# Attention of a graph network on one core: the turned one-hots move from VectorE to ScalarE, and VectorE weighs seven tiles of a block instead of five

## The chip, the cores and the metric

The kernel runs on one core of a Trainium2 chip, as one program in one launch. The metric is the device time of an execution in microseconds. Before the change it is 14080.11 us, the median of four runs (14073.81 to 14083.2).

## What is computed

A graph has 20,000 nodes with 256 features and 340,000 directed edges, self loops among them. Layer 0 is two relational graph convolutions with eight edge types, a residual and a layer norm. Layer 1, which the change touches, is attention with four heads over the edges into each node (`row`) from its neighbours (`col`):

```python
def _gat_forward(x, W, a_l, a_r, edge):
    h = (x @ W).reshape(n, NHEAD, OUT_F)
    hl = jnp.sum(a_l * h, axis=-1)
    hr = jnp.sum(a_r * h, axis=-1)
    e = jax.nn.leaky_relu(hl[row] + hr[col], negative_slope=ALPHA)
    e_max = jax.ops.segment_max(e, row, num_segments=n)
    ee = jnp.exp(e - e_max[row])
    denom = jax.ops.segment_sum(ee, row, num_segments=n)
    att = ee / denom[row]
    msg = att[:, :, None] * h[col]
    out_h = jax.ops.segment_sum(msg, row, num_segments=n)
    return out_h.reshape(n, NHEAD * OUT_F)
x = _layernorm(x + _gat_forward(x, W, a_l, a_r, edge_index))
```

The segment maximum and the segment sums are taken over edges that were sorted by `row` beforehand, so that a block of 128 nodes has its edges together.

## The kernel before

`rounds` does layer 0 and the sorting; `attention` does layer 1. Attention goes over 157 blocks of 128 nodes. A block has up to 17 tiles of 128 edges (`T3`), and an 18th "tile" for the self loops. In a tile the edges lie on the partitions.

For each tile of a block the kernel needs the same relation, "edge e belongs to node p", in three shapes:

- `s` (line 1386, VectorE): edges on the partitions, nodes along the row, 1 or 0 in fp32. It is the weight of the matmul that sums the messages by node (`sums`, line 1474).
- `pen` (`distances`, line 1380, ScalarE): nodes on the partitions, edges along the row, in bf16: the square of (own node - p) times a huge constant, so 0 where the edge belongs to node p and enormous elsewhere. `greatest` (line 1418, VectorE) subtracts it from the scores and takes the maximum of a row, which gives each node the greatest score of its own edges.
- `st` (`turned_hots`, line 1392, VectorE): nodes on the partitions, edges along the row, 1 or 0 in bf16, made from `ob`, the own nodes of the edges spread over all partitions. It is the weight of the matmul that brings a node's terms back to its edges (`spread`, line 1438).

`pen` is made in three parts of 6, 6 and 5 tiles. `greatest` runs twelve times for a block, three parts by four heads: TensorE writes the scores of one head to `pr` (line 1415; two buffers), and VectorE reduces them.

The messages are the gathered rows `g` of the neighbours, 256 numbers wide, times the four attention weights of their edge. This weighing is divided: VectorE does tiles 0 to 4 in two instructions (`weigh_few`, line 1466, 2 and 3 tiles), ScalarE the others with four instructions of 64 columns for each tile (`weigh`, line 1460).

The order is written out by hand (`tc.manual_schedule()`), engine by engine. `step(i)` works on three blocks at once: block a = i gets its penalties, maxima and one-hots; block b = i - 1 gets its weights, is weighed and its first sums are taken; block c = i - 2 gets its last sums, is finished, normed (in lots of four blocks, `write`) and written. After c's last sum, `sums(c, [17])`, its `g` buffer is free (there are four), and GpSimd starts the 17 indirect gathers of block c + 4 (`load`, line 1358). SP's queue carries the `ob` loads of block i + 2 (line 1342), the block's own `g` rows, `xb` and the output. Within a step the loop over n from 1 to 9 sets side by side one sum of TensorE, the weighing of a tile by ScalarE and one reduction of VectorE:

```python
for n in range(1, 10):
    if a and n in (1, 3):
        distances(a, (n + 1) // 2)
    if b:
        sums(b, [n])
...
        if not few or n in (1, 4, 7):
            weigh(b, [n + 4])
        if n == 9:
            weigh(b, [14, 15])
    if a:
        greatest(a, (n + 2) // 4, (n + 2) % 4)
        if n == 5:
            turned_hots(a)
```

`few` is true for the last block alone, which has fewer than eight tiles.

Of the kernel before, what the change touches and what calls it, by code (L numbers as in the profile page):

```python
# [35 lines left out]
BF16 = mybir.dt.bfloat16  # L36
# [3 lines left out]
AF = mybir.ActivationFunctionType  # L40
ALU = mybir.AluOpType
# [6 lines left out]
P = 128  # L48
# [9 lines left out]
T3 = 17  # L58
# [16 lines left out]
def gnn_kernel(  # L75
# [17 lines left out]
    nc = tc.nc  # L93
# [83 lines left out]
    ones = const.tile([P, P], F32, name="ones")  # L177
# [8 lines left out]
    row_of = const.tile([P, 1], F32, name="row_of")  # L186
# [1118 lines left out]
    def attention(words):  # L1305
        with tc.tile_pool(name="ac", bufs=1) as cp, tc.tile_pool(name="ag", bufs=4) as gp, \
# [20 lines left out]
            parts = [(q, min(6, T3 - q)) for q in range(0, T3, 6)]  # L1327
# [35 lines left out]
            def others(k):  # L1363

                n = k["n"]
                k["ob"] = obs.pop(k["b"])
                k["pen"] = sp.tile([P, T3, P], BF16, name="pen")
                k["hpt"] = turns[k["b"] % 2]

                k["top"] = sp.tile([P, H, 1 + len(parts)], F32, name="top")  # L1370
                nc.scalar.copy(k["top"][:, :, 0], k["g"][:, n, D:SR])
                k["hl"] = sp.tile([P, 2, H], F32, name="hl")
                nc.scalar.copy(k["hl"][:, 0, :], k["g"][:, n, SR:SR + H])

            def distances(k, i):

                q, m = parts[i]
                m = min(m, k["n"] - q)
                if m > 0:
                    nc.scalar.activation(k["pen"][:, q:q + m], k["ob"][:, q:q + m], AF.Square, bias=away, scale=FAR)  # L1380

            def one_hots(k):

                s = k["s"] = sp.tile([P, T3, P], F32, name="s", bufs=3)
                n = k["n"]
                nc.vector.tensor_tensor(s[:, :n], pi.unsqueeze(1).to_broadcast([P, n, P]),
                                        own3[:, k["b"], :n].unsqueeze(2).to_broadcast([P, n, P]), op=ALU.is_equal)

            def turned_hots(k):

                k["st"] = sp.tile([P, T3, P], BF16, name="st")
                nc.vector.tensor_scalar(k["st"][:, :k["n"]], k["ob"][:, :k["n"]], row_of, None, op0=ALU.is_equal)  # L1392

            def ends(k, i):

                q, m = parts[i]
                m = min(m, k["n"] - q)
                if m <= 0:
                    return
                ph = p2.tile([P, 6, P], F32, name="pr")  # L1400
                for t in range(q, q + m):
                    nc.tensor.matmul(ph[:3 * H, t - q, :], k["g"][:, t, SR + H:].bitcast(BF16), identb,  # L1402
                                     start=True, stop=True)
                nc.scalar.copy(k["hpt"][:3 * H, q:q + m, :], ph[:3 * H, :m, :])  # L1404
# [19 lines left out]
            def own_terms(k):  # L1424
                z = sp.tile([P, H], F32, name="z")
                nc.vector.tensor_reduce(z, k["top"][:, :, :1 + -(-k["n"] // 6)], op=ALU.max, axis=AX.X)
                hl = k["hl"]
                nc.vector.tensor_add(z, z, hl[:, 0, :])
                nc.vector.scalar_tensor_tensor(hl[:, 1, :], z, SLOPE, z, op0=ALU.mult, op1=ALU.max)
                k["hlp"] = split(sp, hl.rearrange("p a h -> p (a h)"), [2 * H], "hlp")  # L1430

            def spread(k):

                k["pe"] = p1.tile([P, 512], F32, name="pe")
                n = k["n"]
                pe = k["pe"][:, :(n + 1) * 6 * H].rearrange("p (t c) -> p t c", t=n + 1)
                for t in range(n + 1):
                    nc.tensor.matmul(pe[:, t], k["st"][:, t, :] if t < n else identb, k["hlp"], start=True, stop=True)  # L1438
# [14 lines left out]
            def weigh(k, ts):  # L1453

                for t in ts:
                    if t > k["n"]:
                        return
                    gh = k["g"][:, t, :D].rearrange("p (h f) -> p h f", h=H)
                    for h in range(H):
                        nc.scalar.activation(gh[:, h, :], gh[:, h, :], AF.Copy, scale=k["g"][:, t, D + h:D + h + 1])  # L1460

            def weigh_few(k, ts):

                t, n = ts[0], len(ts)
                gh = k["g"][:, t:t + n, :D].rearrange("p t (h f) -> p t h f", h=H)
                nc.vector.tensor_mul(gh, gh, k["pw"][:, t:t + n, :].unsqueeze(3).to_broadcast([P, n, H, HF]))  # L1466

            def sums(k, ts):
                n = k["n"]
                for t in ts:  # L1470
                    if t == 0:
                        k["po"] = p2.tile([P, SR], F32, name="po")
                    if t <= n:
                        nc.tensor.matmul(k["po"], k["s"][:, t, :] if t < n else ident, k["g"][:, t, :SR],  # L1474
                                         start=(t == 0), stop=(t == n))
# [39 lines left out]
            def step(i):  # L1515

                a, b, c = (blocks.get(x) for x in (i, i - 1, i - 2))
                if b:  # L1520
                    own_terms(b)
                if a:
                    others(a)
                    ends(a, 0)
                    distances(a, 0)
                if c:
                    sums(c, [11, 12])
                    weigh(c, [16])
                if b:
                    spread(b)  # L1530
                if a:
                    one_hots(a)
                if c:
                    sums(c, [13])
                if a:
                    ends(a, 1)
                if c:
                    weigh(c, [17])
                    sums(c, [14])
                if a:  # L1540
                    ends(a, 2)
                if c:
                    sums(c, [15, 16])
                if b:
                    load_x(b)
                if b and not a:

                    weights(b)
                    for t in range(0, b["n"] + 1, 6):
                        weigh_few(b, list(range(t, min(t + 6, b["n"] + 1))))  # L1550
                        sums(b, range(t, min(t + 6, b["n"] + 1)))
                    if c:
                        sums(c, [17])
                        finish(c)
                        measure(c)
                        write(c)
                    finish(b)
                    measure(b)
                    write(b)
                    return  # L1560
                if b:
                    weights(b)
                    weigh_few(b, [0, 1])
                    weigh_few(b, [2, 3, 4])
                if a:
                    greatest(a, 0, 0)
                if c:
                    sums(c, [17])
                    if c["b"] + 4 < NB:
                        blocks[c["b"] + 4] = load(c["b"] + 4)  # L1570
                load_ob(i + 2, 0)
                if a:
                    greatest(a, 0, 1)
                if b:
                    sums(b, [0])
                if a:
                    greatest(a, 0, 2)
                if c:
                    finish(c)
                few = a and a["n"] < 8  # L1580
                for n in range(1, 10):
                    if a and n in (1, 3):
                        distances(a, (n + 1) // 2)
                    if b:
                        sums(b, [n])
                        if few and n in (1, 4, 7):
                            weigh_few(b, [n + 5, n + 6])
                        if not few or n in (1, 4, 7):
                            weigh(b, [n + 4])
                        if n == 9:  # L1590
                            weigh(b, [14, 15])
                    if a:
                        greatest(a, (n + 2) // 4, (n + 2) % 4)
                        if n == 5:
                            turned_hots(a)
                    if n in (2, 4, 6, 8):
                        load_ob(i + 2, n // 2)
                    if c and n == 1:
                        measure(c)
                    if c and n == 4:  # L1600
                        write(c)
                if b:
                    sums(b, [10])
# [330 lines left out]
```

## Time and profile before

| what | value |
|---|---|
| median of the runs | 14080.11 us |
| the profiled execution, its time | 14087.55 us |
| its span | 14085.8 us |
| mean granted TensorE clock | 0.857 |
| busy over the span: TensorE, VectorE, ScalarE, GpSimd | 71%, 54%, 42%, 54% |
| 11,000 to 12,000 us, in attention, busy: TensorE, VectorE, ScalarE, GpSimd | 545, 558, 563, 471 us |
| the same 1,000 us: granted clock, DMA share | 0.77, 0.36 |

The page of a profile gives each engine's busy time, the span in 40 slices, the DMA queues, the chain that ended last and the costliest groups of instructions. A row of a group has the line of the code, the engine, the operation, what it writes and reads, how often it ran, its busy time, the mean duration of one in ns, and the idle time of the engine in front of it with what ended that idle time. A row in order of time has its start, its duration and, in brackets, the idle time in front of it and its releaser; "issue" stands for a wait that nothing in the profile explains, "remote" for one that a semaphore ended whose sender isn't known. Two durations that overlap on one engine are an instruction's end and the next one's start; the distance from start to start is what an instruction costs there.

### The profile page before, as it was taken

What the parts mean: (1) busy time and instruction counts of PE and PEld (TensorE: products, weight loads), DVE (VectorE), ACT (ScalarE), POOL (GpSimd) and SP (SyncE); (2) the same over time, 40 slices, a digit from 0 to 9 for tenths busy, and PEclk for the clock granted to TensorE, in tenths of its full rate; (3) what the DMA queues carried; (4) which work ended last, traced back from release to release, by engine and by line L of the source; (5) the groups of instructions that cost most, each with busy time, mean ns of one, the idle gap of its engine ahead of it and who ended that gap; (6) DMA issues with size and microseconds to landing.
All of it is one profiled execution on the core that took longest, in us unless ns stands there. A gap on an engine that the chain in (4) does not pass through costs nothing. (4 is left out here: it accounts for less than half of the span.)

```text
span 14085.8 us, 220738 instructions
## 1 busy us (share of the span) xinstructions
PE 9939.7 (71%) x75815; PEld 7494.0 (53%) x75815; DVE 7570.8 (54%) x21335; ACT 5967.3 (42%) x18175; POOL 7630.3 (54%) x8041
## 2 busy tenths in 40 slices
PE   7788888888877888887888885555555555555555
PEld 6677766666666666666666663333333333333333
DVE  4455555555554555555555543555555555555556
ACT  2311114444443333333333332555555555555555
POOL 6666666665655555555555554444444444444443
PEclk8999989999998999999999997777777777777777
DMA  5655545554545454555555553333333333333332
GB/s 170 203 144 144 144 140 143 142 142 140 143 136 143 141 142 141 145 145 143 142 143 144 144 149 102 97 99 97 94 98 96 98 95 95 95 100 96 97 96 81
DMA packets 860286, 1777.61 MB, mean 126 GB/s; under 512 B 196892, under 2 KB 525834, under 8 KB 859130
## 3 DMA queue, kind: packets, MB, share of 16 engines
q0 software_dynamic: 461200, 1384.74, 35.9%
q1 hardware_dynamic: 390098, 371.45, 8.5%
q8 instruction: 596, 9.76, 0.3%
q10 hardware_dynamic: 7848, 7.20, 0.2%
q14 instruction: 544, 4.46, 0.1%
HBM read 1629.85 MB, written 132.98 MB: 125 GB/s over the span
## 5 line engine op out<-in xcount | busy, mean ns | idle before, releaser
L1358 POOL DMA_INDIRECT g<-table3s,words x2657 | 2539.9, 956 | 2893.0 <-PE po L1474 2067.1
L611 POOL DMA_INDIRECT g<-h2s,idx x2657 | 2519.9, 948 | 1886.6 <-PE a L731 1017.9
L731 PE MATMUL a<-s,g 128*128 128x152 bf16 (+9 forms) x34860 | 2950.4, 229 | 135.7 <-issue 111.4
L678 PE MATMUL pm<-wt,to 128*128 128x256 f32 x10624 | 3018.3, 408 | 16.0 <-issue 12.4
L611 POOL DMA_INDIRECT g<-xs,idx x2209 | 2105.1, 953 | 1362.9 <-PE a L731 686.9
L1418 DVE CUSTOM_DVE_ANT_0 dump<-pr,pen 128x768 bf16<-128x768 f32 x1876 | 1660.5, 910 | 2113.1 <-remote 1495.1
L1415 PE MATMUL pr<-hpt,pick 128*128 128x512 bf16 (+2 forms) x3752 | 1025.4, 360 | 2356.6 <-DVE top L1418 1291.2
L731 PEld LDWEIGHTS <-g 128*128 128x128 bf16 x32844 | 2230.8, 101 | 452.6 <-issue 209.4
L1460 ACT ACTIVATE g<-g 128x64 f32<-128x64 f32 x8088 | 2086.9, 334 | 572.3 <-issue 566.7
L1474 PE MATMUL po<-g,s 128*128 128x260 f32 x5314 | 1970.9, 468 | 85.3 <-DVE g L1466 85.3
L678 PEld LDWEIGHTS pm<-wt,to 128*128 128x128 f32 x10624 | 1888.9, 198 | 236.9 <-issue 55.8
L1415 PEld LDWEIGHTS <-pick 128*128 128x128 bf16 x3752 | 395.9, 106 | 2941.1 <-issue 2821.1
L656 ACT COPY to<-a 128x512 f32<-128x512 f32 x996 | 555.7, 585 | 2757.2 <-PE a L731 2109.5
L1145 DVE CUSTOM_DVE_ANT_0 dump<-pr,b 128x157 f16<-128x157 f32 x2657 | 713.2, 320 | 1869.2 <-PE pr L1125 684.8
L969 DVE TENSOR_TENSOR b<-pi,kb 128x471 f16<-128x471 f32 (+1 forms) x1798 | 1111.0, 634 | 295.8 <-PE pr L1010 92.2
L1135 ACT ACTIVATE two<-b,words 128x157 f16<-128x157 f16 x2657 | 1122.0, 422 | 291.6 <-DVE b L969 131.4
L1474 PEld LDWEIGHTS po<-g,s 128*128 128x128 f32 x5314 | 978.6, 223 | 497.3 <-issue 223.9
L1136 ACT ACTIVATE two<-b,words 128x157 f16<-128x157 f16 x2657 | 1101.3, 414 | 0.0
L1404 ACT CAST hpt<-pr 12x768 bf16<-12x768 f32 (+1 forms) x469 | 350.0, 747 | 1507.7 <-PE pr L1402 1504.7
L634 DVE TENSOR_TENSOR s<-pi,code 128x1216 bf16<-128x1216 f32 x610 | 860.9, 1412 | 0.0
L674 PE MATMUL pm<-wt,ot 128*128 128x256 f32 x1328 | 478.5, 494 | 423.7 <-issue 281.7
L1163 PE MATMUL pl<-two,a 128*128 128x314 f16 x2657 | 540.4, 314 | 266.4 <-DVE a L1151 199.3
(290 smaller groups left out, 10756.9 us busy)
## 6 DMA issues: line engine op xcount, KB each, us to landing
ob<-ownd SPq DMA_DIRECT2D x625, 128.0 KB
g<-h2s,idx POOLq DMA_INDIRECT x2657
g<-table3s,words POOLq DMA_INDIRECT x2657
g<-xs,idx POOLq DMA_INDIRECT x2209
h2s<-h SPq DMA_DIRECT2D x166, 192.0 KB
own<-h2s SPq DMA_DIRECT2D x166, 192.0 KB
xs<-xs SPq DMA_DIRECT2D x156, 192.0 KB
own<-xs SPq DMA_DIRECT2D x136, 192.0 KB
```

Of the source, the lines that this page charges most:

```text
L611: nc.gpsimd.indirect_dma_start(out=g, out_offset=None, in_=of, in_offset=bass.IndirectOffsetOnAxis(ap=idx[u // CS][:, u % CS:u % CS + 1], ...
L634: nc.vector.tensor_tensor(s, pi[:, :w].unsqueeze(1).to_broadcast([P, e - f, w]), codes(c, e - f).unsqueeze(2).to_broadcast([P, e - f, w]), ...
L678: nc.tensor.matmul(p, to[:, i % 2, i // 2, :P], wt[:, i % 2, i // 2, :], start=False, stop=(i == 2 * R - 1))
L731: nc.tensor.matmul(a[h, q][:, b:e, :].rearrange("p n r -> p (n r)"), g[:, v * D + h * P:v * D + (h + 1) * P], s, start=((h, q) not in begu ...
L969: nc.vector.tensor_tensor(b[:, :n], pi[:, :NB].unsqueeze(1).to_broadcast([P, n, NB]), self.k["kb"][:, c:c + G * (n - 1) + 1:G].unsqueeze(2 ...
L1135: nc.scalar.activation(two[:, 0, :], made[m][:, x, :], AF.Copy, scale=k["hi"][:, c:c + 1])
L1136: nc.scalar.activation(two[:, 1, :], made[m][:, x, :], AF.Copy, scale=k["lo"][:, c:c + 1])
L1358: nc.gpsimd.indirect_dma_start(out=g[:, t, :], out_offset=None, in_=table3s, in_offset=bass.IndirectOffsetOnAxis(ap=to3[:, b, t:t + 1], ax ...
L1415: nc.tensor.matmul(pr[:, t:t + n, :], pick[:, h, :], k["hpt"][:, q + t:q + t + n, :], start=True, stop=True)
L1418: nc.vector.tensor_tensor_reduce(out=dump[:, :m, :].rearrange("p t e -> p (t e)"), in0=pr[:, :m, :].rearrange("p t e -> p (t e)"), in1=k[" ...
L1460: nc.scalar.activation(gh[:, h, :], gh[:, h, :], AF.Copy, scale=k["g"][:, t, D + h:D + h + 1])
L1474: nc.tensor.matmul(k["po"], k["s"][:, t, :] if t < n else ident, k["g"][:, t, :SR], start=(t == 0), stop=(t == n))
```

## The change

`st` is no longer made by VectorE from `ob` in one instruction, but by ScalarE from `pen` in three, one for each part: max(0, 1 - pen), which is 1 where the penalty is 0, and 0 elsewhere. These stand at n = 2, 4 and 6. VectorE weighs seven tiles in two instructions (3 and 4 tiles) instead of five, and ScalarE begins at tile 7. For the last block alone the order of the weighing is adapted.

```diff
-            def turned_hots(k):
+            def turned_hots(k, i):
-                k["st"] = sp.tile([P, T3, P], BF16, name="st")
-                nc.vector.tensor_scalar(k["st"][:, :k["n"]], k["ob"][:, :k["n"]], row_of, None, op0=ALU.is_equal)
+                q, m = parts[i]
+                m = min(m, k["n"] - q)
+                if i == 0:
+                    k["st"] = sp.tile([P, T3, P], BF16, name="st")
+                if m > 0:
+                    nc.scalar.activation(k["st"][:, q:q + m], k["pen"][:, q:q + m], AF.Relu, bias=ones[:, 0:1],
+                                         scale=-1.0)
...
-                    weigh_few(b, [0, 1])
-                    weigh_few(b, [2, 3, 4])
+                    weigh_few(b, [0, 1, 2])
+                    weigh_few(b, [3, 4, 5, 6])
...
-                        if few and n in (1, 4, 7):
+                        if few and n in (4, 7):
                             weigh_few(b, [n + 5, n + 6])
-                        if not few or n in (1, 4, 7):
+                        if few and n == 1:
+                            weigh(b, [7])
+                        if n > 2 and not few or n in (4, 7):
                             weigh(b, [n + 4])
...
-                        if n == 5:
-                            turned_hots(a)
+                        if n in (2, 4, 6):
+                            turned_hots(a, n // 2 - 1)
```

## The prediction

> **What bounds the kernel now.** I read the page's 40 slices first: the attention stage is the part from about 8,660 us to the end, and there no engine is busy for more than 56 to 57% (1,000 us from 11,000: VectorE 558, ScalarE 563, TensorE 545, GpSimd 471). So it is a stage of waits, and the view to read is who waits for whom. For VectorE, between 9,500 and 13,500 us (116 steps, one per block of 128 nodes, so 34.5 us a step):
>
> ```profile
> DVE dump L1418 <- remote: 1113.8, 230, 8.8
> DVE dump L1418 <- issue: 334.9, 66, 8.2
> ...
> DVE dump L1418 <- PE pr L1415: 113.4, 137, 2.0
> ```
>
> The columns are total us, times, longest. All three are the reductions of `greatest`, twelve a step, which I call r0 to r11. Together that is 1562.1 / 116 = 13.5 us a step, and "remote" and "issue" say that the profile can't name what ended the wait. Next the instructions in order of time, for one step, VectorE and then TensorE:
>
> ```profile
> 11018.62 0.96 DVE L1418 CUSTOM_DVE_ANT_0 dump<-pr,pen 128x768 bf16<-128x768 f32 x1 [2.02 <-PE pr L1415]
> ...
> 11026.37 0.96 DVE L1418 CUSTOM_DVE_ANT_0 dump<-pr,pen 128x768 bf16<-128x768 f32 x1 [6.78 <-issue]
> ...
> 11027.25 0.78 DVE L1392 TENSOR_SCALAR st<-ob,row_of 128x2176 bf16<-128x2176 bf16 x1
> 11032.79 0.83 DVE L1418 CUSTOM_DVE_ANT_0 dump<-pr,pen 128x640 bf16<-128x640 f32 x1 [4.76 <-issue]
> ```
>
> ```profile
> 11019.64 0.43 PE L1415 MATMUL pr<-hpt,pick 128*128 128x512 bf16 x2 [2.06 <-DVE top L1418]
> ...
> 11027.39 0.69 PE L1415 MATMUL pr<-hpt,pick 128*128 128x512 bf16 x2 [6.41 <-issue]
> ```
>
> These are r6, r7, the one-hots `st` that the change takes away, and r8. TensorE made r8's input at 11019.64; r8 starts at 11032.79. In this stretch VectorE's news reaches TensorE at once (r7's input slot is refilled 0.13 us after r7's result), but TensorE's news reaches VectorE 2 to 13 us late. ScalarE is slow in it too: its 64-wide multiplications start every 0.24 us up to 11019.2 and every 0.71 us after it. What else runs then are the 17 gathers of the block four steps on:
>
> ```profile
> 11008.60 0.95 POOL L1358 DMA_INDIRECT g<-table3s,words  x1 [13.68 <-PE po L1474]
> ...
> 11027.40 1.45 POOL L1358 DMA_INDIRECT g<-table3s,words  x1 [0.30 <-issue]
> ```
>
> Call the first gather's start g. Over the 138 full steps between 8,900 and 13,900 us I read the start of each reduction against g. r5 starts at g+7.0, without a wait; r6, r7 and r8 come late; and the last reduction that waited over 0.9 us starts at g+24.2 (median; three quarters of the steps lie under g+24.25, 95% under 24.29). That moment does not follow the last gather's start, which moves from g+20.0 to g+20.5 (correlation 0.2). Where there are no gathers, at the end, the one-hots `s` of two steps stand 19.8 us apart, and VectorE is filled:
>
> ```profile
> 14035.00 2.42 DVE L1386 TENSOR_TENSOR s<-pi,words 128x2176 f32<-128x2176 f32 x1
> ...
> 14054.77 0.82 DVE L1386 TENSOR_TENSOR s<-pi,words 128x640 f32<-128x640 f32 x1
> ```
>
> So the step is: g, 24.2 us of stretch in which few reductions get through, then what is left of them and the chain to the next g. The time is set by how many are left at g+24.2: steps with r9 left last 33.05 us, with r8 left 34.55, or 33.85 where r8 came through 0.7 us before the restart.
>
> **The change, part by part.** The durations:
>
> ```profile
> L1380 ACT ACTIVATE pen<-ob,away 128x768 bf16<-128x768 bf16 x232 | 214.5, 924 | 0.0
> ...
> L1466 DVE TENSOR_TENSOR g<-g,pe 128x768 f32<-128x768 f32 x116 | 109.9, 947 | 0.0
> ...
> L1392 DVE TENSOR_SCALAR st<-ob,row_of 128x2176 bf16<-128x2176 bf16 x116 | 93.8, 809 | 0.0
> ...
> L1466 DVE TENSOR_TENSOR g<-g,pe 128x512 f32<-128x512 f32 x116 | 79.9, 689 | 141.9 <-ACT pe L1450 141.9
> ```
>
> *`st` leaves VectorE:* one instruction, 0.81 us, 0.70 from its start to the next. It stands between r7 and r8, inside the stretch, and r8 waits 3.6 us behind it on average; what hides it is that wait, so it is worth nothing there. It is worth 0.70 us only where r8 starts the moment `st` ends; I count 8 of the 138 steps, and 8 x 153/138 x 0.70 = 6 us.
>
> *Two more tiles are weighed by VectorE:* a third tile costs 947 - 689 = 0.26 us, so two cost 0.52 us. They stand in front of r0, where VectorE does not wait, so r0 to r5 all come 0.52 us later and r5 moves to g+7.56. g does not move: TensorE reaches the sum that frees the gathers' buffer without `weigh_few` of this block. The price shows only in the stretch. The trace has such a delay: every fourth step (class 3) reloads ScalarE's table for Exp (1.28 us) and has r5 at g+8.48, 1.44 us later than class 0. There r6 is 3.0 us later, r7 4.65 us (g+21.5 against 16.8), and r8 only 0.65 us (24.37 against 23.72), because the restart cuts it off. 0.52/1.44 of 0.65 is 0.23 us a step, over the 153 steps with gathers 36 us. From below it is 0: if the restart rules alone, nothing moves. Class 3 differs in more than this delay, so I take 0.1 us, 15 us, nearer to the lower end.
>
> *ScalarE:* 8 multiplications go (7.73 us for 32 of them, 0.24 each: 1.9 us), three max(0, 1 - penalty) come. They are of the form of the row L1380 (same widths, a bias of one value per partition), which takes 0.82, 0.82 and 0.72 us from start to start: 2.36 us. So ScalarE has 0.45 us more. It lies beside ScalarE's idle time in front of the next `hpt` copy, 13.0 us in this step and 9.0 in the one before; without that cover it would cost 0.45 x 157 = 71 us. The penalties read were written at least one instruction earlier, and the number of table loads does not change.
>
> *New wait:* TensorE's `spread` of the next step now waits for ScalarE's one-hots. Behind it stand the last sums of the block before, and with them g. ScalarE's last work of the step starts at 11024.23, `spread` at 11038.10: 13.9 us of cover, so 0. SP's first `ob` load no longer waits for VectorE; it follows 0.4 us behind SP's `g` load, which waits for TensorE, so 0.
>
> *ScalarE sends less in front of the stretch:* by g+8 it starts 27 instructions instead of 34. If its traffic is part of what fills the stretch, that is a gain. The nearest row is class 2, where ScalarE stands waiting for Sqrt and has started 12 fewer (22.6): r6 at 8.1, r7 at 12.1, r8 at 21.1, step 33.58 us against 34.44. But in these steps SP has also moved only 576 of the 1,008 packets of `ob` by then. So 7/12 x 0.86 x 153 = 77 us is the lower end, 0 the upper; I take 0, since 432 packets are the larger difference.
>
> *GpSimd:* 43 of the 44 gathers that lasted over 1.1 us overlap `st`, as the 1.45 us above. Without it the last gather starts 0.15 us earlier on average: 0 if the restart does not follow it (correlation 0.2), 23 us if it does. I take 0. The Trainium skill ("Advanced Engine Details and Errata", VectorE Performance Modes) says that VectorE's second SBUF port is shared with GpSimd and that the two block each other; the longer gathers agree. By that rule alone the sum would be 23 us lower.
>
> The Trainium skill also has a rule against the change ("ScalarE: Activation LUTs", Rules for kernel authors): max and relu belong on VectorE, up to about three times faster in bf16. The rows agree, 0.81 us against 2.36. The rule would make the step 1.55 us dearer; here neither side stands on the path.
>
> **The sum.** +15 - 6, and in the last four steps, where VectorE is full, 4 x (0.52 - 0.70) = -1: +8 us. The profiled execution took 14087.55 us (span 14085.8) and would take 14,096; the median of the runs shown, 14080.11, is 0.05% lower, so I forecast 14,088.
>
> **Rivals.** *Faster:* the thinner ScalarE lets one more reduction through before the restart in many steps. For it: class 2. Against it: class 2's `ob` packets. In full 77 us: 14,003. *Slower:* the 0.52 us in front of r0 pushes r6 to r8 further into the stretch, and r8 meets the restart. It decides from r8 starting after g+23.4, where a step loses its r9 restart (1.5 us; 25 of 35 in class 2, few elsewhere), or the 0.7 us of an early r8. In full: class 0 loses 24.24 - 23.72 = 0.52, class 1 0.18, class 2 25/35 x 1.5 = 1.07, class 3 a late r7 of about 0.3; the mean is 0.52, times 153 is 79 us: 14,159. For it: class 3; against it: r8 is already at the restart in most steps. *It does what it says and it counts:* VectorE's 0.17 us less would be the step's if VectorE were the bound, 27 us: 14,053, inside the forecast's case. Only the last four steps are like that.
>
> **How the numbers follow.** A measurement of this kernel can tell about 0.2%, 28 us, from no change. The forecast's case, 14,052 to 14,108, gets 0.42; the faster rival 0.27; the slower 0.31, since the delay is certain and the relief is not. The range takes in both rivals in full: 14,000 to 14,160.
>
> **What would show it.** `st` on ScalarE, three instructions of 0.92, 0.92 and 0.81 us; the 4-tile `weigh_few` at about 1.2 us; r5 at g+7.56; the restart still at g+24.2; no gather over 1.1 us. The prediction is wrong if the restart moves, if the share of steps with r8 begun before g+23.4, which restart with r9 (30 of 138), changes by more than a tenth, or if `spread` waits for ScalarE.

## The result, and the profile after

The changed kernel takes 14104.41 us (median of 36 runs) against 14082.43 us of the kernel before (56 runs): 1.0018 times as long, 95% interval 1.0013 to 1.0023, that is some 22 us or 0.14 us in each of the 153 steps with gathers. The forecast was 14,088 us, with no change by over 0.2%.

The kernel before takes 13,913 to 14,087 us in some groups of runs (these, e1 to e4, and e14 with e15: the *long* condition) and 10,205 or 10,210 us in others (e6, e8, e10, e11, and e12 with e13: the *short* condition), so the time of each experiment is compared only with the kernel before of its own group.

The page of the changed kernel, its span and its engines:

```profile
span 14132.4 us, 219609 instructions
...
PE 9984.1 (71%) x75815; PEld 7522.7 (53%) x75815; DVE 7546.1 (53%) x21177; ACT 5989.3 (42%) x17404; POOL 7610.8 (54%) x8041
```

VectorE's busy time fell from 7570.8 to 7546.1 us (one-hots off, two tiles on), 0.16 us a step, as reckoned. ScalarE's rose from 5967.3 to 5989.3, 22 us, where 0.45 us in 157 steps would be 71. Both moves are small. The profiled execution is 46.6 us above the one of before (14085.8); the medians differ by 22, so this execution lies in the upper part of its runs and its differences are to be read as larger than the usual ones. The waits of VectorE, of the same 4,000 us as in the prediction (114 steps):

```profile
DVE dump L1423 <- remote: 1002.9, 204, 9.0
DVE dump L1423 <- issue: 476.9, 104, 7.6
...
DVE dump L1423 <- PE pr L1420: 113.4, 159, 2.0
```

The three together are 1593.2 / 114 = 14.0 us a step, 13.5 before. So VectorE has 0.17 us less to do in a step and waits 0.5 us more. Where it waits, one step in order of time shows; its first gather starts at 10995.48, and the rows are r5, r6, r7 and r8:

```profile
11005.44 0.96 DVE L1423 CUSTOM_DVE_ANT_0 dump<-pr,pen 128x768 bf16<-128x768 f32 x1 [0.89 <-PE pr L1420]
...
11011.82 0.96 DVE L1423 CUSTOM_DVE_ANT_0 dump<-pr,pen 128x768 bf16<-128x768 f32 x1 [5.42 <-issue]
...
11019.55 0.96 DVE L1423 CUSTOM_DVE_ANT_0 dump<-pr,pen 128x768 bf16<-128x768 f32 x1 [6.76 <-remote]
...
11020.43 0.82 DVE L1423 CUSTOM_DVE_ANT_0 dump<-pr,pen 128x640 bf16<-128x640 f32 x1
```

It is a step that begins with a reload of the table for Exp, the prediction's class 3. r5 starts at g+9.96 and now waits itself; r6 waits 5.4 us, and the wait of 6.8 us that ends at g+24.1 is in front of r7. In the step shown in the prediction r7 was through by then and r8 stood there. One more reduction is left when the stretch ends. The means over the trace, by kind of step, from one start of `s` to the next (a write step holds the output's normalisation; the reload step follows it):

| mean step, us | reload | next | next but one | write | all |
|---|---|---|---|---|---|
| steps in the prediction | class 3 | class 0 | class 1 | class 2 | |
| before | 35.38 | 34.46 | 34.75 | 33.59 | 34.55 |
| after | 36.63 | 34.43 | 34.88 | 33.39 | 34.83 |

The loss is in the reload steps: 1.25 us in each of 37. Among 149 steps the end of the stretch meets r7 in 29 (before: 3), r8 in 82 (113) and r9 in 38 (33); it lies at g+24.20 (24.22). The 29 are all reload steps.

### The profile page after: what moved, and what is told of

Its sections match the earlier page's. It is cut to its first block, busy times and chain, and to the rows that moved or that the text cites. A ratio compares the mean times of both kernels' runs of the same rounds, so it can differ in the third digit from the quotient of the medians.

```text
span 14132.4 us, 219609 instructions
## 1 busy us (share of the span) xinstructions
PE 9984.1 (71%) x75815; PEld 7522.7 (53%) x75815; DVE 7546.1 (53%) x21177; ACT 5989.3 (42%) x17404; POOL 7610.8 (54%) x8041
## 5 line engine op out<-in xcount | busy, mean ns | idle before, releaser
L1465 ACT ACTIVATE g<-g 128x64 f32<-128x64 f32 x6848 | 1755.5, 333 | 283.0 <-issue 280.6
```

## The experiments

**Theory A**, from the prediction: what the two more tiles put in front of VectorE's first reduction is the loss. **Rival B**: ScalarE's added work is. The runs e1 to e4 are one group, in the long condition (kernel before 14087.41 us). In e1 and e3 the function `turned_hots` is that of the change; the diffs show the rest, and "..." stands for lines left out.

The figures "before" of a single step or a wait all come from the one profiled execution of the kernel before, which belongs to the first group. The part ahead of attention, which no edit touches, differs between the profiled executions: attention's first gather starts at 8639.5 us before, and at 8620.5, 8620.2, 8637.2 and 8608.1 in e1 to e4. Such differences come to as much as 31 us, 0.2 us for each of 153 steps, so a mean over steps that differs by 0.2 us or less between two executions shows little by itself.

**e1_st_only**: the one-hots on ScalarE, five early tiles as before.

```diff
...
-                        if n == 5:
-                            turned_hots(a)
+                        if n in (2, 4, 6):
+                            turned_hots(a, n // 2 - 1)
```

> The kernel before, with only the first part of the change: the turned one-hots are made by ScalarE in three instructions, and VectorE goes on weighing five tiles early. Theory A (the loss is the 0.52 us that the two extra tiles put in front of VectorE's first reduction; ScalarE's part is hidden): nothing is added in front of the first reduction and 0.81 us leaves VectorE behind the ninth, so 0 to 10 us below the kernel before, and the first tile's reduction stays about 7.0 us behind the first gather. Rival B (the loss is ScalarE's added 2.36 us, which delays its waiting work in the next step): 20 to 70 us above the kernel before, since here ScalarE gives up no tile for it.

Measured: 14092.87 us, 1.0003 (0.9993 to 1.0012). Rival B as stated, 20 to 70 us, falls: 2.36 us of work a step added to ScalarE, with nothing taken away, cost 5 us in all, between -10 and +17. A smaller part of ScalarE's is not excluded: in the one profiled execution the write steps last 34.24 us against 33.59, and the end of the stretch meets r9 in 20 of 149 steps instead of 33. The 0.70 us taken from VectorE brought no gain that shows. The waits of VectorE in 115 steps:

```profile
DVE dump L1423 <- remote: 1250.8, 235, 9.6
DVE dump L1423 <- issue: 252.6, 43, 8.9
...
DVE dump L1423 <- PE pr L1420: 127.8, 155, 2.0
```

"Remote" and "issue" are 13.07 us a step against 12.49 before: VectorE waits 0.58 us more where it works about 0.64 us less. This fits the prediction's "worth nothing there".

**e2_seven_only**: seven early tiles, the one-hots still on VectorE.

```diff
-                    weigh_few(b, [0, 1])
-                    weigh_few(b, [2, 3, 4])
+                    weigh_few(b, [0, 1, 2])
+                    weigh_few(b, [3, 4, 5, 6])
...
```

> The kernel before, with only the second part of the change: VectorE weighs seven tiles early, and goes on making the turned one-hots itself. Theory A (0.52 us in front of the first reduction costs about 0.15 us a step): 20 to 35 us above the kernel before, most of it in the steps that follow a write of the output, where the exponentials' table is loaded anew; the sixth reduction about 7.55 us behind the first gather instead of 7.0. Rival B (ScalarE's part): within 5 us of the kernel before, or below it, since ScalarE only gets thinner here.

Measured: 14121.5 us, 1.0027 (1.0018 to 1.0037), 34 us above the kernel before (25 to 52), at the upper end of theory A. r5 comes at g+7.57 (7.03 before; 0.52 was expected). By kind of step it is 36.82 in reload steps (+1.44), 34.51 and 35.02 in the next two, and 32.91 in write steps (-0.68). The means point to two effects: the delay costs in the reload steps, and ScalarE, 1.9 us thinner and with the one-hots not put on it, lets more through in the write steps: in 14 of 149 steps r9 too is done when the stretch ends, in none before. The second is the prediction's faster rival; it is seen only there (e1, with ScalarE 2.36 us fuller, has the write steps 0.65 us longer), and the first outweighs it.

The two halves of the change add up to 5 + 34 = 39 us, the change itself to 22. With 13 us to either side of each half and 7 of the change, that difference is not shown to be more than noise.

**e3_two_late**: the one-hots on ScalarE, and VectorE weighs two more tiles, but the thirteenth and fourteenth, behind r7.

```diff
...
-                        if not few or n in (1, 4, 7):
+                        if not few and n < 8 or n in (1, 4, 7):
                             weigh(b, [n + 4])
...
+                    if b and not few and n == 5:
+                        weigh_few(b, [12, 13])
```

> Both parts of the change, but the two extra tiles are other ones (the thirteenth and fourteenth) and VectorE weighs them between the eighth and the ninth reduction, where it waits anyhow, so that nothing is put in front of the first reduction. Theory A (what counts is when VectorE begins the reductions): 0 to 15 us below the kernel before. Rival C (work on VectorE counts wherever it stands, 0.95 us for two tiles less 0.81 for the one-hots): about 20 us above the kernel before, as the change. Rival D (two tiles in the wait push the ninth reduction past the end of the wait): 30 to 100 us above.

Measured: 14083.76 us, 0.9996 (0.9987 to 1.0005). As much work on VectorE and on ScalarE as in the change (but for the tile widths), in another place, and no loss shows. (ScalarE, too, is relieved late in the step here and not early as in the change. e3 alone does not separate the two, but in e2 an early relief went with a gain, in the write steps.) Rivals C and D fall: r5 is back at g+7.03, reload steps at 35.35, and the two tiles stand in the wait:

```profile
DVE dump L1423 <- remote: 859.8, 156, 9.0
DVE dump L1423 <- issue: 583.0, 126, 9.1
...
DVE dump L1423 <- PE pr L1420: 136.7, 153, 2.1
```

"Remote" and "issue" are 12.55 us a step (115 steps), 0.52 less than in e1 (13.07), which hasn't got the two tiles: the wait is shorter by most of the 0.69 us that two tiles in one instruction take.

**e4_three**: the other way, three early tiles instead of five, all else as before.

```diff
-                    weigh_few(b, [0, 1])
-                    weigh_few(b, [2, 3, 4])
+                    weigh_few(b, [0, 1, 2])
+                    weigh(b, [3, 4])
```

> The kernel before, with VectorE weighing three tiles early instead of five, ScalarE the other two; the turned one-hots stay on VectorE. Theory A (each half microsecond in front of the first reduction is worth 0.15 us a step): VectorE begins about 0.5 us earlier, 15 to 30 us below the kernel before. Rival B (ScalarE decides: two more tiles are 1.1 us on it, and the fourth and fifth weighed tile come later to TensorE): 20 to 70 us above. Rival E (five is where the two effects meet): within 10 us.

Measured: 14012.18 us, 0.9950 (0.9936 to 0.9963), 75 us below the kernel before. Theory A has the sign; the size is over twice what was expected. Not all of it need come from the steps: the profiled execution is 80 us shorter than that of the kernel before, and 31 of these lie ahead of attention's first gather, 49 behind it (34.23 against 34.55 us a step). r5 comes at g+6.46, and the end of the stretch meets r9 in 103 of 149 steps instead of 33: the steps after the reload step fall to 33.37 and 33.92, while write and reload steps gain nothing (33.84, 35.79).

e1 and e4, of one group, side by side are the clearest reading. The busy time of the engines between 9,500 and 13,500 us, of e1 and then of e4; columns are the window, its length, and then PE, PEld, VectorE, ScalarE and GpSimd, the granted clock, the DMA share and GB/s:

```profile
9500.00:13500.00 4000.00, 2168.84 (x10921) 1234.74 (x10921) 2137.84 (x5231) 2526.79 (x7676) 1847.98 (x1955) 0.77 0.35 96
```

```profile
9500.00:13500.00 4000.00, 2233.86 (x11108) 1273.38 (x11108) 2185.53 (x5320) 2577.90 (x8376) 1897.04 (x1985) 0.75 0.36 97
```

VectorE has 2137.84 / 115 = 18.6 us of work a step in e1 and 2185.53 / 117 = 18.7 in e4, against 2230.14 / 116 = 19.2 before; ScalarE has 22.0 in both. The same load on both engines, and 81 us between the two times; between the two profiled executions, too, 81 us lie behind attention's first gather. What differs is where the work lies: VectorE's in front of r0 and, with it, ScalarE's (two more tiles instead of the one-hots). That VectorE's part decides is argued from r5, which comes 0.57 us earlier in e4 (g+6.46 instead of 7.03), and from the reductions left.

**e14_after_again and e15_after_exp**, one group, long condition (kernel before 13912.77 us): the changed kernel once more, and with an exponential of one column behind each write, so that the table is loaded there.

```diff
                     nc.sync.dma_start(out[b * P:b * P + n, :], o[:n])
+                back = sp.tile([P, 1], F32, name="back")
+                nc.scalar.activation(back, eps, AF.Exp)
```

> The changed kernel again, beside the next one. On a chip with the long wait in the steps: 20 to 30 us above the kernel before, as found. On a chip without it (the kernel before at 10,205 us): no reduction waits out a long stretch there, so Theory A foresees no loss from a later beginning; what counts is the busier of VectorE and ScalarE: VectorE gives 0.81 us and takes 0.95 us, ScalarE takes 2.36 us and gives 1.9 us a step, so within 35 us of the kernel before, to either side.

> The changed kernel with the early exponential behind a write, again, beside the changed kernel on one chip. On a chip with the long wait, Theory A: the steps after a write come down from 36.75 us to the 34.4 to 34.9 of the plain ones, 50 to 90 us below the changed kernel; rival F (the table's load only moves): within 15 us of it. On a chip without it: the 31 us below the kernel before of the first look, and against the changed kernel the 1.3 us that a load of the table takes, in 39 steps, at most 50 us.

Measured: 13931.49 us, 1.0011 (1.0003 to 1.0020), and 13908.17 us, 0.9996 (0.9987 to 1.0005). The change costs 19 us here too. The early exponential gives 23 us back, and with that all that the change lost, but it is less than half of the 50 to 90 expected, and more than rival F's 15. The load did move (line 1455 is the step's Exp, 1518 the added one; first e14, then e15):

```profile
L1455 ACT ACT_TABLE_LOAD x29 | 37.2, 1283 | 0.5
```

```profile
L1518 ACT ACT_TABLE_LOAD x29 | 37.2, 1283 | 0.5
```

and the reload steps came down, from 35.78 to 34.59, but the step after them rose from 33.76 to 34.19, the others being 34.30 and 33.11 in e14, 34.34 and 33.17 in e15. In these two executions, then, a reload step had been followed by a short one, and I had counted only the long one. No step of e15 is left with r7 (8 in e14).

The next ones were meant for the long condition and fell into the short one; apart from the kernel of e15, what they were to tell apart in the long one was not tried.

**e6_after_exp**, the kernel of e15, and **e10_three_exp**, e4 with the same exponential (kernel before of this group: 10204.91 us).

> The changed kernel, with one exponential of a single column behind the four normalisations of a write, so that the exponentials' table is loaded there, and not at the start of the step that follows, in front of the first reduction. Theory A (the loss of the change sits in the steps after a write, 36.75 us against 34.41 to 34.85 in the plain ones, because there the reductions begin latest): these 39 steps come down by about 2 us each, 50 to 90 us below the changed kernel, and so 30 to 65 us below the kernel before. Rival F (the load of the table only moves to where ScalarE is needed as much): within 15 us of the changed kernel.

> The kernel before with three early tiles on VectorE instead of five (75 us below the kernel before, alone), and the early exponential as well. Theory A: both begin VectorE's reductions earlier in front of the same wait; the steps after a write, still 35.87 us against 33.4 to 33.9 in the others with three tiles, come down to these, so another 60 to 90 us: 130 to 170 us below the kernel before. Rival F (the table's load only moves): 60 to 90 us below, as with three tiles alone.

Measured: 10173.57 us, 0.9968 (0.9956 to 0.9980), and 10202.99 us, 0.9996 (0.9987 to 1.0005). What was worth 75 us in the long condition is worth nothing here. In this condition the step is another one. GpSimd's group of gathers between 7,300 and 9,900 us, first e6, then e10:

```profile
L1358 POOL DMA_INDIRECT g<-table3s,words x2076 | 1968.4, 948 | 633.3 <-issue 599.3 <-PE pr L1420 11.6 <-DVE top L1423 5.5
```

```profile
L1358 POOL DMA_INDIRECT g<-table3s,words x2049 | 1976.8, 965 | 624.5 <-issue 602.2 <-DVE top L1418 11.6 <-DMA g<-table3s,words 6.1
```

The gathers stand end to end, each behind a gap of 0.30 us: 17 of them are 17 x 2600 / 2076 = 21.3 us in e6 and 21.6 in e10, and the step is 21.39 and 21.59 us. GpSimd is the bound. And here one gather takes 965 ns where VectorE makes `st` and 948 where ScalarE does: 17 x 17 ns = 0.29 us a step. Of the gathers of e10 that take over 970 ns, those that overlap `st` hold 303 of 307 ns of lengthening a step; e6 has 46 ns in all. So the prediction's term for GpSimd, 0 to 23 us, which I took as 0, counts where the gathers are the bound; the 0.20 us between the two steps are 31 us over 153, and 29 us lie between the two times. e6 and e10 differ in the early tiles too, so this is argued from the gathers' durations, not shown by a run of that one part alone. The Trainium skill ("Advanced Engine Details and Errata", VectorE Performance Modes), with its second SBUF port that VectorE and GpSimd share, agrees with these rows; it speaks for the change, and in the long condition the wait hid it.

**e11_one**, one early tile on VectorE, in the same group.

```diff
-                    weigh_few(b, [0, 1])
-                    weigh_few(b, [2, 3, 4])
+                    weigh_few(b, [0])
+                    weigh(b, [1, 2, 3, 4])
```

> The kernel before with one early tile on VectorE instead of five; ScalarE weighs the other four. Theory A, carried on: VectorE begins about 1 us earlier than in the kernel before, with more reductions in front of the wait, 80 to 150 us below the kernel before. Rival B (ScalarE becomes what is late: it had 433 us of idle time left before the turned scores in 4,000 us with three tiles, 3.7 us a step, and two more tiles are 1.1 us of it at its free rate, more in the wait): between the three-tile kernel and the kernel before, or above it.

Measured: 10361.81 us, 1.0153 (1.0139 to 1.0167). Rival B is right in the short condition: the step is 22.57 us, and the chain that ended last in the whole execution goes 32% over ScalarE, 21% over line 1460, the weighing. Whether one tile would do better than three in the long condition stays open.

**e8_half_plain and e13_half_again**: the kernel before with every second gather replaced by a plain load of as many bytes, always of the same rows in a block; it leaves out half of the gathering.

```diff
                 for t in range(m):
+                    if b >= 4 and t % 2:
+                        nc.sync.dma_start(g[:, t, :], table3s[b * P + 1:(b + 1) * P + 1, :])
+                        continue
                     nc.gpsimd.indirect_dma_start(
```

> The kernel before with the gathers of every second tile (8 of 17, from the fifth block on) replaced by plain loads of as many bytes, of one and the same set of rows in a block; it leaves out half of the gathering, and its output is not the reference's. Theory A's ground (the wait in the step is made by the gathers while GpSimd issues them, not by the bytes): VectorE's reductions go on again about 12 to 14 us behind the first gather instead of 24.2, and a step comes near VectorE's own 20 to 24 us: 1,400 to 2,000 us below the kernel before. Rival G (the bytes, or something in the step that is not the gathers): within 300 us of the kernel before, going on again at 24 us.

> The same kernel as the one with half of the gathers replaced by plain loads, which met a chip on which the kernel before takes 10,205 us and has no long wait in its steps. If this chip is one of the kind of the first runs (14,080 us for the kernel before): Theory A's ground (the long wait is made by the gathers while GpSimd issues them): the reductions go on again about 12 to 14 us behind the first gather instead of 24.2, the step near 21 us, and 1,400 to 2,000 us below the kernel before. Rival G (bytes, or the chip's own slowness): within 300 us, the wait still ending at 24 us. If it is of the faster kind, the 70 us of the first look again.

Measured, one run each: 10135.63 us (kernel before 10204.91) and 10136.57 us (10210.45). Both fell into the short condition, so the ground of theory A, that the gathers make the long wait, was not tested. What they show is how near the next bound is: GpSimd, of the second of them, now waits for buffers,

```profile
POOL g L1361 <- PE po L1477: 1210.9, 122, 12.9
```

10 us a step, and the step is only 0.4 us shorter (21.12) than e12's, below, where the gathers bound it. VectorE is busy for 2324.5 and ScalarE for 2297.1 of 2,600 us, so these two come next.

**e12_three_late_exp**: e10, and VectorE weighs the thirteenth and fourteenth tile behind r8, in the group of e13.

```diff
-                        if not few or n in (1, 4, 7):
+                        if not few and n < 8 or n in (1, 4, 7):
                             weigh(b, [n + 4])
...
+                    if b and not few and n == 6:
+                        weigh_few(b, [12, 13])
```

> The kernel before with three early tiles on VectorE instead of five, the early exponential behind a write, and the thirteenth and fourteenth tile weighed by VectorE behind the ninth reduction; the turned one-hots on VectorE. On a chip with the long wait, Theory A: VectorE begins earlier in all steps and the two late tiles stand in the wait, so 100 to 170 us below the kernel before, below the 75 us of three tiles alone; rival D (the late tiles, 0.95 us, hold the tenth reduction up): 40 to 75 us below. On a chip without the wait (the kernel before at 10,205 us), where VectorE and ScalarE are 80 to 90% busy in this stage: as many tiles on VectorE as before, so only the table's load moves, 0 to 35 us below the kernel before.

Measured: 10201.97 us, 0.9990 (0.9981 to 0.9999), within what was expected of the short condition. The step is 21.56 us with gathers of 965 ns, as in e10: where the tiles stand brought no difference while GpSimd was the bound.

So e4 beats both kernels in the long condition, and e6, which holds the change, beats the kernel before in the short one. No version was seen to do both; e12 was not run in the long condition, and the change alone not in the short one.

## Why the prediction was right, point by point

- **What bounds the step:** right in the long condition. The stretch ends at g+24.2 in the kernels of e1 to e4 as in both others, and the mean step follows how many reductions are left then (e4: r9 in 103 of 149 steps, step 34.23; before: 33, 34.55; after: r7 in 29 steps, 34.83). In e14 and e15 the stretch ends a little earlier, near g+24.0. "So it is a stage of waits" holds for that condition only.
- **`st` leaves VectorE, -6 us:** not contradicted. e1 has +5 (-10 to +17) for this and ScalarE's part together.
- **Two more tiles in front of r0, +15 of 0 to 36:** the place was right, the size too low, and the way from the delay to the loss was another. e2 shows 34 us, and 22 with the one-hots moved; 0.14 to 0.22 us a step where I took 0.1. I had priced it by how much later r8 starts in class 3, cut off by the restart. The loss is a whole reduction more that is left at the restart, r7, and only in the reload steps. The prediction has this in the slower rival, too small: "class 3 a late r7 of about 0.3". In the reload steps r5 came 0.9 us later rather than 0.52, because r5 itself now waits, and r7 was left behind: 1.25 us a step. That the bound of 36 us came near e2's 34 is therefore luck. Class 2, which I had losing 1.07, lost nothing and won 0.2; class 0 and class 1, 0.52 and 0.18, lost nothing and 0.13. The slower rival's total, 79 us, was wrong in three of four kinds of step.
- **ScalarE +0.45 us hidden, no new wait:** right within e1's interval. The `hpt` copy waited 1333.2 us for TensorE in the 4,000 us after (1111.7 before), and TensorE's loads of `st` in `spread` have no wait for ScalarE among theirs, only 23.5 us of "issue" (17.9 before). TensorE's first sum of a block does wait 0.79 us instead of 0.54 (89.7 us in 114 steps, 62.0 in 115), which fits the first `weigh_few`, 0.95 us instead of 0.69; the row names ScalarE's `pen`, which ends within 0.1 us of it. No cost of this shows apart from the others.
- **ScalarE thinner, 0 of up to -77:** in the change 0 is nearly right, the write steps have 0.20 us less. e2, with more taken from ScalarE, has 0.68 less there.
- **GpSimd, 0 of up to -23:** right in the long condition, for the reason given: the end of the stretch does not follow the last gather. "No gather over 1.1 us" was wrong: 105 of 2,470 are, 41 before; the mean of a gather is 954 ns, 955 before. Now it is the fifth of a step, and what stands beside it is VectorE's sum of `o` and `xb`, which the longer early weighing moved onto the gather's start:

```profile
11035.26 0.95 POOL L1358 DMA_INDIRECT g<-table3s,words  x1 [0.30 <-issue]
11036.41 0.42 DVE L1490 TENSOR_TENSOR o<-o,xb 128x256 f32<-128x256 f32 x1
11036.51 1.14 POOL L1358 DMA_INDIRECT g<-table3s,words  x1 [0.30 <-issue]
11036.75 0.95 DVE L1423 CUSTOM_DVE_ANT_0 dump<-pr,pen 128x768 bf16<-128x768 f32 x1
```

A reduction beside it is not what lengthens it: in the reload steps, where that sum comes later, the fifth gather lies beside a reduction as well and takes 0.95 us. In the short condition the prediction's term for GpSimd is the one that counts.

- **What would show it:** r5 at g+7.57, the stretch's end at g+24.20, the share of steps with r8 begun before g+23.4 at 38 of 149 (33 before): as foreseen, if "a tenth" is a tenth of all steps (22% to 26%). That share was the wrong thing to watch alone, since the loss came from r7. `st` on ScalarE has the durations named; the 4-tile `weigh_few` too (the last figure is the longest, in ns):

```profile
L1471 DVE TENSOR_TENSOR g<-g,pe x228: 953/1085/1215, 9531.3 to 13471.1; 128x768 f32<-128x768 f32 x114
...
L1396 ACT ACTIVATE st<-pen,ones x344: 811/917/922, 9501.7 to 13484.6; 128x768 bf16<-128x768 bf16 x115, 128x640 bf16<-128x640 bf16 x57
```

So the forecast was right because the parts that it put at nothing were worth little in sum, and the one that it put at 15 us was worth about 22. In part it was luck: by kind of step the losses and gains were others than the prediction's, and they partly cancelled. The verdict of "no change by 0.2%" was near its edge.

## What to carry to other kernels

Where a chain of work has to get through before a wait that ends at a fixed moment, look at where added work stands: here about 0.5 us more in front of r0 cost 34 us (e2), 0.57 us less brought up to 75 (e4), and 0.69 us behind r7 cost nothing that shows (e3). Work out the price for each kind of step, by whether one more link falls behind the wait or comes through: the delay cost in the reload steps, which were latest already, and the advance paid in the steps after them. And before a step is tuned around a wait of which the profile cannot name the cause, see whether the wait is always there: here it was gone in two groups of runs, and with it the value of the best edit.

## What the runs showed of the hardware that I had not expected

- The two conditions. The kernel before takes 14,082, 14,087 or 13,913 us in some groups of runs and 10,205 or 10,210 us in others; within a group its runs lie within 0.5%. Two groups recorded ten minutes apart bear the same chip number and show both, 10,210.45 us and 13,912.77 us, so the chip alone does not seem to decide. Nor is it a matter of attention alone: attention's first gather starts at 8639.5 us in the kernel before and at 6784.3 in e12, so of the 3,882 us between these two executions 1,855 lie ahead of attention, in code that is the same in both. In the short condition VectorE's wait for the reductions is nearly gone. Here is e12, between 7,300 and 9,900 us (121 steps); these are all its waits in front of reductions:

```profile
DVE dump L1418 <- PE pr L1415: 64.8, 74, 2.0
```

That is 0.5 us a step instead of 13.5, and the gathers of a block no longer wait for their buffer (1544.3 us in the 4,000 us of the kernel before). The gathers themselves go at one pace in both: 17 of them start within 20.2 us in the kernel before and 20.3 in e12 (means). So the gathers alone do not make the long wait. The granted clock goes with it, 0.97 in e12's row against 0.75 to 0.77 in the two rows of e1 and e4, though TensorE is busier in e12:

```profile
7300.00:9900.00 2600.00, 1996.39 (x11461) 1160.42 (x11458) 2297.00 (x5603) 2271.13 (x7706) 1975.60 (x2049) 0.97 0.56 154
```

The clock is too small for the difference: a step of 34.5 us and one of 21.6 have a ratio of 1.60, the clocks 1.26, and VectorE's and ScalarE's single instructions last the same (a reduction 0.95 us; the weighing starts every 0.24 us in e12, and so it does in the kernel before outside the stretch, whereas inside it the 0.71 us from start to start are one instruction of 0.35 and idle time). The transfers took as long in both: the packets of the gathers' queue hold 35.9% of 14,085.8 us and 48.7% of 10,203.9, which is 5,057 and 4,969 us. So in the long condition it is mostly the waits that are longer, and not the work. What brings it about, no run here shows.
- A gather that overlaps VectorE's `st` takes longer: 965 against 948 ns in the mean of all gathers of a step. One that starts beside the sum of `o` and `xb` takes 1.14 us instead of 0.95. No cost of either shows in the long condition; where the gathers stand end to end, about 0.2 us a step go with the first.
- A reload step that was made shorter by moving 1.28 us of table load out of it (35.78 to 34.59) made the next one longer (33.76 to 34.19).
